# Routed results scaled by ScalarE and scattered to two token tables; a step's sum formed by accumulating transfers

## The chip, the cores and the metric

The kernel runs on one core of one Trainium2 chip. The metric is the device time of one execution in microseconds (us). Three runs of the kernel before gave a median of 2758.53 us (2753.56 to 2760.92). PE is TensorE, DVE VectorE, ACT ScalarE, POOL GpSimd, and SP the engine that here only issues transfers. A transfer issued from POOL goes through the software queue (q0 in the profile), one issued from SP through the hardware queue q1, one issued from ACT through q10.

## The reference

Two sequences of 4096 tokens, 512 features, float32. First a recurrent layer (a weight matrix `W` of 512x512 per sequence, updated after each token), a residual and a layernorm. Then a feed-forward layer with one shared and eight routed experts, a residual and a second layernorm:

```python
logits = einsum('btd,ed->bte', X, routing_W) + expert_bias
activation = sqrt(softplus(logits))
top_vals, top_idx = top_k(activation, 2)
combine = sum(one_hot(top_idx, 8) * top_vals[..., None], axis=-2)     # weight of each expert per token
y = silu(X @ rW1[e] + rb1[e]) @ rW2[e] + rb2[e]                       # for every expert e
routed = einsum('ne,end->nd', combine, y)
return layernorm(X + shared(X) + routed)
```

Each token uses two experts, so a kernel need compute only two of the eight `y`, and sum them with their weights.

## The kernel before

**Steps.** The 4096 tokens of a sequence are cut into 32 steps `c` of 128 tokens; a step holds both sequences, `B = 2`, so 256 tokens. `step(c)` (L392 on) is the recurrent layer in chunk form, with the update of `W` at L457 (matmul `pw`) and L458 (VectorE adds it to `W`), of the bias at L463 and L464 (`pb`, `brep`), and the residual at L452 and L453 (`po`, `x`). `prep(c+1)` and `invert(c)` prepare a triangular inverse: `invert` is a chain of small VectorE instructions (L347) that ends in the tiles `D` and `DT` (L364); `join` begins with a matmul `pn` that needs `D` (L376). `shared(c-1)` does the shared expert (its result added at L620) and `router(c-1)` the choice of two experts.

**Groups, tiles and tables.** Steps 0 to 22 are group a, steps 23 to 30 group b (`GROUPS = (23, 8)`); step 31 is done with all eight experts densely (`dense`, L644 to L675). For each chosen expert of each token, `router` writes the token's number (4 bytes) into one of four DRAM tables `gt` at a place that belongs to the expert (L557, four scatters of a step). At a group's end `plan` (L678) reads the tables back and cuts the pairs of token and expert into tiles of 128, 99 for group a and 39 for group b. `routed` (L759) runs over the tiles: gather 128 token rows `g` from DRAM (L766), gather the expert's weights `wb` of 1.3 MB (L772; left out by index where the buffer has them already), transpose (`pg`, L781), first layer (`phe`, L790, and ACT's silu into `he`, L794), second layer (`pye`, L801), add the bias on VectorE into `o` (L804), and write `o` with a plain SP transfer to its place in the DRAM tensor `ge` (L806), which is in order of tiles. `o` has two buffers, `g` three, `wb` three.

**Collecting.** `collect` (L827) takes one step of a group at a time: load `acc` (512 KB, shared expert plus residual, L834), gather for each of two sequences and two chosen experts the 128 result rows from `ge` into a tile `z` (256 KB each, L840), and on VectorE add each `z` times its weight `cw` to `acc` (L857). Then layernorm (`bn_stats` at L276, a square root on ACT at L281, scale and shift on ACT at L287) and the output, an ACT transfer `y_out` (L867). `plan` works out the rows of `ge` for each token, `sidx` (L732 to L744).

**Order.** Generators are interleaved by hand with `interleave`, which always resumes the part with the smallest share done. The order of PE and VectorE is exactly the order of the code; that of ACT, POOL and SP is set by a scheduler at build time. Each engine runs its own list in order, and a wait at its head holds back all that is behind it. Group a's tiles are spread over steps 24 to 27; its collection runs in steps 28 to 31, five steps in each of the first three and three in the last, and the other five beside group b's tiles. Then comes the dense expert work of step 31, with the eight collections of group b beside it:

```python
    interleave([(b.tiles * TILE, tiles[1]), (60.0, shared(NCH - 1)),
                ((a.n - sum(COLLECTED.values())) * COLLECT, collects[0])])
    dense_weights(E - len(dense_w))
    interleave([(DENSE, dense(NCH - 1)), (b.n * COLLECT, collects[1])])
```

Of the kernel before, what the change touches and what calls it, by code (L numbers as in the profile page):

```python
# [39 lines left out]
F32 = mybir.dt.float32  # L41
# [6 lines left out]
P = 128  # L48
# [5 lines left out]
K = 2  # L54
# [47 lines left out]
def postln_block(ctx: ExitStack, tc: tile.TileContext, x, xT, thK, thV, thQ, w0, b0, masks, blk,  # L102
# [24 lines left out]
    cp = ctx.enter_context(tc.tile_pool(name="cp", bufs=2))  # L127
# [99 lines left out]
    class Group:  # L227
# [9 lines left out]
        def begin(self):  # L237
            g = self.g

            def d(tag, shape):  # L240
                return dram.tile(shape, F32, tag=f"{tag}{g}", name=f"{tag}{g}", bufs=1)

            self.y, self.base = d("gy", [self.rows, D]), d("gb", [self.rows, D])

            self.tables = [d(f"gt{i}", [E * self.cap, 1]) for i in range(B * K)]
            self.ex = d("ge", [self.tiles * P, D])
            zero = plp.tile([P, E * self.cap // P], F32, tag="big", name=f"zero{g}")
            nc.vector.memset(zero, 0.0)
            for table in self.tables:
                nc.sync.dma_start(out=table.rearrange("(p n) o -> p (n o)", p=P), in_=zero)  # L250

            def t(tag, shape, dt=F32):
                return plp.tile(shape, dt, tag=f"{tag}{g}", name=f"{tag}{g}")

            i = plp.tile([P, E], I32, tag="iota", name=f"i_first{g}")
            nc.gpsimd.iota(i, pattern=[[self.cap, E]], base=0, channel_multiplier=0)
            self.first = t("first", [P, E])
            nc.vector.tensor_copy(self.first, i)
            self.next = t("next", [P, E])
            nc.vector.tensor_copy(self.next, self.first)  # L260
            self.cw = t("cw", [P, self.n, B, K])
            self.row = t("row", [P, self.n, B, K])
            self.widx = t("widx", [P, self.tiles], I32)
            self.gidx = t("gidx", [P, self.tiles], I32)
            self.sidx = t("sidx", [P, self.n, B, K], I32)
# [207 lines left out]
    def router(c, yT):  # L473
# [75 lines left out]
        for what, to in ((place, gr.row), (act, gr.cw)):  # L549
            v = small("selv", (P, B, K, E))  # L550
            nc.vector.tensor_tensor(v, sel, what[:, :, None, :].broadcast_to(full), ALU.mult)
            nc.vector.tensor_reduce(to[:, j], v, AX.X, ALU.add)
        ri = sm.tile([P, B, K], I32, tag="ri", name=f"ri_{c}")
        nc.vector.tensor_copy(ri, gr.row[:, j])  # L554
        for s in range(B):
            for k in range(K):
                nc.gpsimd.indirect_dma_start(  # L557
                    out=gr.tables[s * K + k],
                    out_offset=bass.IndirectOffsetOnAxis(ap=ri[:, s, k:k + 1], axis=0),
                    in_=code[:, j * B + s:j * B + s + 1], in_offset=None,  # L560
                    bounds_check=E * gr.cap - 1, oob_is_err=False)
# [116 lines left out]
    def plan(gr):  # L678
# [38 lines left out]
        for i in range(0, NT, half):  # L717
# [13 lines left out]

        step = tmp("step", [P, E - 1])  # L732
        nc.vector.tensor_scalar(step, tiles[:, 0:E - 1], float(P), float(-CAP),
                                ALU.mult, ALU.add)
        n = gr.n * B * K
        full = [P, n, E - 1]
        rows = gr.row.rearrange("p n s k -> p (n s k)")
        adj = tmp("big", full, "adj")
        nc.vector.tensor_tensor(adj, rows[:, :, None].broadcast_to(full),
                                gr.first[:, None, 1:].broadcast_to(full), ALU.is_ge)  # L740
        nc.vector.tensor_tensor(adj, adj, step[:, None, :].broadcast_to(full), ALU.mult)
        sl = tmp("sl", [P, n])
        nc.vector.tensor_reduce(sl, adj, AX.X, ALU.add)
        nc.vector.tensor_tensor(gr.sidx.rearrange("p n s k -> p (n s k)"), sl, rows, ALU.add)  # L744
        codes = tmp("big", [NT, B * K, P], "codes")
        for i, table in enumerate(gr.tables):
            nc.gpsimd.indirect_dma_start(
                out=codes[:, i, :], out_offset=None, in_=table.rearrange("(r n) o -> r (n o)", n=P),
                in_offset=bass.IndirectOffsetOnAxis(ap=r32[0:NT, 0:1], axis=0),
                bounds_check=E * CAP // P - 1, oob_is_err=False)  # L750
        yield 8.0
        ps = ps_f.tile([P, NT], F32, tag="pf", name=f"pc_{g}")
        for i in range(B * K):
            nc.tensor.matmul(ps, codes[:, i, :], ident[0:NT, 0:NT], start=(i == 0),
                             stop=(i == B * K - 1))
        nc.vector.tensor_copy(gr.gidx, ps)
        yield 0.2

    def routed(gr):  # L759

        NT = gr.tiles
        g_t, gT, h_t = {}, {}, {}
# [34 lines left out]
        def second(k):  # L797
# [7 lines left out]
            v = gr.order[k]  # L805
            nc.sync.dma_start(out=gr.ex[v * P:(v + 1) * P], in_=o)  # L806
# [8 lines left out]
        for k in range(NT):  # L815
            if k + NW < NT:
                tokens(k + NW)
            hidden(k)
            if k + 1 < NT:
                turn(k + 1)  # L820
            yield 2.5
            second(k)
            if k + NW < NT:
                weights(k + NW)
            yield 2.0

    def collect(gr):  # L827

        got = {}

        def fetch(j):
            c = gr.c0 + j
            acc = cp.tile([P, B, D], F32, tag="acc", name=f"acc_{c}", bufs=3)
            nc.gpsimd.dma_start(out=acc,  # L834
                                in_=gr.base[j * T:(j + 1) * T].rearrange("(s p) d -> p s d", p=P))
            z = []
            for s in range(B):
                for k in range(K):
                    t = cp.tile([P, D], F32, tag=f"z{s}{k}", name=f"z_{c}_{s}_{k}")
                    nc.gpsimd.indirect_dma_start(  # L840
                        out=t, out_offset=None, in_=gr.ex,
                        in_offset=bass.IndirectOffsetOnAxis(ap=gr.sidx[:, j, s, k:k + 1], axis=0),
                        bounds_check=gr.tiles * P - 1, oob_is_err=False)
                    z.append(t)
            got[j] = acc, z

        fetch(0)
        yield 2.0
        for j in range(gr.n):
            c = gr.c0 + j  # L850
            if j + 1 < gr.n:
                fetch(j + 1)
            acc, z = got.pop(j)
            norm = []
            for s in range(B):
                for k in range(K):
                    nc.vector.scalar_tensor_tensor(acc[:, s, :], z[s * K + k],  # L857
                                                   gr.cw[:, j, s, k:k + 1], acc[:, s, :],
                                                   ALU.mult, ALU.add)
                    yield 0.8  # L860
                norm.append(layernorm(acc, "f", c, s, scalar=True))
                next(norm[s])
                yield 0.4
                if s > 0:
                    next(norm[s - 1])
            next(norm[B - 1])
            nc.scalar.dma_start(out=out[:, c * P:(c + 1) * P, :].rearrange("s p d -> p s d"),  # L867
                                in_=acc)
# [109 lines left out]
```

## Time and profile before

| | |
|---|---|
| device time, median of three runs | 2758.53 us (2753.56 to 2760.92) |
| the profiled execution: device time, and its span from first to last instruction | 2757.97 us, 2756.0 us |
| mean granted TensorE clock of the profiled execution | 0.989 |
| busy share of the span: PE, DVE, ACT, POOL | 96%, 47%, 27%, 28% |
| group a's tiles | 1540 to 2191 us, PE busy 636.8 of 651 us |
| steps 28 to 31 with collections of group a | 2191 to 2474 us, PE busy 255.3 of 283 us |
| group b's tiles | 2474 to 2677 us, PE busy 179.5 of 203 us |
| dense experts and collections of group b | 2677 to 2756 us, PE busy 59.1 of 79 us |
| bytes moved by transfers | 269.42 MB |

The page gives busy times per engine, idle time before groups of instructions with what ended it, and for transfers the time from issue to landing. The four stretches of the table have different limits, so shares over the whole span say little about the change: it touches the last 1216 us.

### The profile page before, as it was taken

What the parts mean: (1) busy time and instruction counts of PE and PEld (TensorE: products, weight loads), DVE (VectorE), ACT (ScalarE), POOL (GpSimd) and SP (SyncE); (2) the same over time, 40 slices, a digit from 0 to 9 for tenths busy, and PEclk for the clock granted to TensorE, in tenths of its full rate; (3) what the DMA queues carried; (4) which work ended last, traced back from release to release, by engine and by line L of the source; (5) the groups of instructions that cost most, each with busy time, mean ns of one, the idle gap of its engine ahead of it and who ended that gap; (6) DMA issues with size and microseconds to landing.
All of it is one profiled execution on the core that took longest, in us unless ns stands there. A gap on an engine that the chain in (4) does not pass through costs nothing. (4 is left out here: it accounts for less than half of the span.)

```text
span 2756.0 us, 32318 instructions
## 1 busy us (share of the span) xinstructions
PE 2658.1 (96%) x10977; PEld 1718.3 (62%) x10977; DVE 1292.1 (47%) x4093; ACT 755.7 (27%) x1474; POOL 766.5 (28%) x767
## 2 busy tenths in 40 slices
PE   8999999999999999999999999999999999889887
PEld 6666666666666666666666676767667655546664
DVE  2455555444445555544445413223132388773238
ACT  1211122222221122222222322323223133334447
POOL 0121111111111111111112433243342355454445
PEclk9999999999999999999999999999999999999998
DMA  4122212111111211121112534344333467775666
GB/s 161 36 50 61 63 40 41 48 40 40 40 40 42 54 48 48 41 48 40 40 40 56 169 71 126 121 107 135 89 126 101 102 180 197 206 223 197 204 213 225
DMA packets 148787, 269.42 MB, mean 98 GB/s; under 512 B 61180, under 2 KB 62940, under 8 KB 145040
## 3 DMA queue, kind: packets, MB, share of 16 engines
q1 hardware_dynamic: 90608, 139.50, 17.5%
q0 software_dynamic: 49584, 111.61, 14.7%
q10 hardware_dynamic: 8432, 16.25, 1.7%
q8 instruction: 88, 1.44, 0.2%
q14 instruction: 75, 0.61, 0.1%
HBM read 333.37 MB, written 88.64 MB: 153 GB/s over the span
## 5 line engine op out<-in xcount | busy, mean ns | idle before, releaser
L347 DVE SCALAR_TENSOR_TENSOR X<-L,X 128x31 f32<-128x31 f32 (+22 forms) x1472 | 332.7, 274 | 27.5 <-DMA L<-dL 10.5
L557 POOL DMA_INDIRECT gt<-code,ri x124 | 123.7, 998 | 710.7 <-DVE ri L554 682.0
L790 PEld LDWEIGHTS phe<-gT,wb 128*128 128x128 f32 x2208 | 270.7, 194 | 75.4 <-issue 68.9
L804 DVE TENSOR_TENSOR o<-pye,wb 128x512 f32<-128x512 f32 x138 | 95.4, 691 | 452.1 <-PE pye L801 436.6
L790 PE MATMUL phe<-gT,wb 128*128 128x128 f32 x2208 | 273.7, 278 | 16.2 <-DMA wb<-wcat_in,widx 15.5
L801 PE MATMUL pye<-wb,he 128*128 128x512 f32 x552 | 266.8, 605 | 21.1 <-ACT he L794 20.4
L457 PE MATMUL pw<-F,K 128*128 128x512 f32 x512 | 244.6, 608 | 9.6 <-DVE W L458 8.1
L304 PE MATMUL pkq<-xT,thK 128*128 128x256 f32 x1024 | 242.9, 381 | 7.6 <-DMA thK<-thK_in 7.6
L304 PEld LDWEIGHTS pkq<-xT,thK 128*128 128x128 f32 x1024 | 195.3, 191 | 82.2 <-issue 61.6
L304 PE MATMUL pkq<-xT,thQ 128*128 128x256 f32 x1024 | 241.9, 380 | 2.6 <-ACT N L378 2.6
L422 PE MATMUL po<-W,kq 128*128 128x512 f32 x512 | 244.2, 600 | 0.0
L402 PE MATMUL pr<-thV,xT 128*128 128x512 f32 x512 | 241.8, 604 | 0.0
L407 PE MATMUL pr<-W,kq 128*128 128x512 f32 x512 | 240.1, 592 | 0.0
L772 POOL DMA_INDIRECT wb<-wcat_in,widx x138 | 141.9, 1028 | 342.9 <-DVE o L804 138.3
L304 PEld LDWEIGHTS pkq<-xT,thQ 128*128 128x128 f32 x1024 | 188.5, 191 | 40.9 <-issue 17.0
L311 ACT COPY kq<-pkq 128x256 f32<-128x256 f32 x256 | 83.2, 374 | 435.2 <-PE pkq L304 434.6
L794 ACT ACTIVATE he<-phe,wb 128x128 f32<-128x128 f32 x276 | 86.5, 363 | 419.1 <-PE phe L790 418.4
L458 DVE TENSOR_TENSOR W<-pw,W 128x512 f32<-128x512 f32 x256 | 173.4, 688 | 59.1 <-PE pw L457 56.6
L457 PEld LDWEIGHTS pw<-F,K 128*128 128x128 f32 x512 | 91.9, 191 | 141.3 <-issue 86.1
L766 POOL DMA_INDIRECT g<-gy,gidx x138 | 138.2, 1001 | 139.3 <-PE pg L781 115.0
L801 PEld LDWEIGHTS pye<-wb,he 128*128 128x128 f32 x552 | 98.6, 189 | 120.9 <-issue 76.7
L840 POOL DMA_INDIRECT z<-ge,sidx x124 | 136.5, 1101 | 100.8 <-DVE acc L857 33.9
(198 smaller groups left out, 3458.9 us busy)
## 6 DMA issues: line engine op xcount, KB each, us to landing
ge<-o SPq DMA_DIRECT2D x138, 256.0 KB, 2.0
xT<-xT_in SPq DMA_DIRECT2D x32, 512.0 KB, 3.7
x<-x_in SPq DMA_DIRECT2D x32, 512.0 KB, 3.7
L<-dL SPq DMA_DIRECT2D x128, 128.0 KB, 4.5
gy<-x SPq DMA_DIRECT2D x31, 512.0 KB, 2.8
gb<-x SPq DMA_DIRECT2D x31, 512.0 KB, 4.5
acc<-gb POOLq DMA_DIRECT2D x31, 512.0 KB, 5.2
y_out<-acc ACTq DMA_DIRECT2D x31, 512.0 KB, 6.0
```

The source lines that it names most:

```text
L304: nc.tensor.matmul(ps[:, i].rearrange("p s t -> p (s t)"), th[:, dc, (ec + i) * P:(ec + i + 1) * P], xt[:, dc].rearrange("p s t -> p (s t) ...
L347: nc.vector.scalar_tensor_tensor(X[:, h, j + 1:], L[:, j + 1:, j], X[:, h, j:j + 1], X[:, h, j + 1:], ALU.mult, ALU.add)
L402: nc.tensor.matmul(ps, xt[:, dc, s, :], nthV_sb[:, dc, :], start=(dc == 0), stop=False)
L407: nc.tensor.matmul(ps, KQ[:, ec, s, 0, :], W[s][:, ec, :], start=False, stop=(ec == DC - 1))
L422: nc.tensor.matmul(ps, KQ[:, ec, s, 1, :], W[s][:, ec, :], start=(ec == 0), stop=False)
L457: nc.tensor.matmul(ps, K[s][:, ec, :], F[s], start=True, stop=True)
L458: nc.vector.tensor_tensor(W[s][:, ec, :], ps, W[s][:, ec, :], ALU.add)
L766: nc.gpsimd.indirect_dma_start(out=g_t[k], out_offset=None, in_=gr.y, in_offset=bass.IndirectOffsetOnAxis(ap=gr.gidx[:, k:k + 1], axis=0), ...
L772: nc.gpsimd.indirect_dma_start(out=wbuf[k % NW], out_offset=None, in_=wcat, in_offset=bass.IndirectOffsetOnAxis(ap=gr.widx[:, k:k + 1], ax ...
L790: nc.tensor.matmul(ps[:, hc, :], w[:, dc * HF + hc * P:dc * HF + (hc + 1) * P], t[:, dc, :], start=(dc == 0), stop=(dc == DC - 1))
L801: nc.tensor.matmul(ps, h[:, hc, :], w[:, O2 + hc * D:O2 + (hc + 1) * D], start=(hc == 0), stop=(hc == HC - 1))
L840: nc.gpsimd.indirect_dma_start(out=t, out_offset=None, in_=gr.ex, in_offset=bass.IndirectOffsetOnAxis(ap=gr.sidx[:, j, s, k:k + 1], axis=0 ...
```

## The change

The second number in the table `gt`, the weight of the token's expert, travels with the token's number (8 bytes instead of 4), and `plan` reads both back, so that each tile knows for its 128 rows the weight (`cw`, one column for a tile) and the destination row (`sidx`). After the bias is added, ACT multiplies `o` by its weight in place, and POOL scatters the 128 rows to `ge`, which now holds two tables in token order, one for the first and one for the second chosen expert. `collect` no longer gathers: the two halves of `ge` for a step are contiguous, and two POOL transfers of 512 KB add them to `acc` as they are written (`accum_op=ADD`). Loads run up to three steps ahead, with five `acc` buffers instead of three; the eight `z` buffers are gone. The four instructions of `plan` over all tokens of a group (L739 to L744) are gone as well.

```diff
-    cp = ctx.enter_context(tc.tile_pool(name="cp", bufs=2))
+    cp = ctx.enter_context(tc.tile_pool(name="cp", bufs=5))
...
-            self.tables = [d(f"gt{i}", [E * self.cap, 1]) for i in range(B * K)]
-            self.ex = d("ge", [self.tiles * P, D])
+            self.tables = [d(f"gt{i}", [E * self.cap, 2]) for i in range(B * K)]
+            self.ex = d("ge", [K * self.rows, D])
...
             for table in self.tables:
-                nc.sync.dma_start(out=table.rearrange("(p n) o -> p (n o)", p=P), in_=zero)
+                for r in table.rearrange("(h p n) o -> h p (n o)", h=2, p=P):
+                    nc.sync.dma_start(out=r, in_=zero)
...
-        for what, to in ((place, gr.row), (act, gr.cw)):
+        row = small("row", (P, B, K))
+        entry = sm.tile([P, B, K, 2], F32, tag="entry", name=f"entry_{c}")
+        for what, to in ((place, row), (act, entry[:, :, :, 1])):
...
+        for k in range(K):
+            nc.vector.tensor_scalar(entry[:, :, k, 0], code[:, j * B:(j + 1) * B],
+                                    float(k * gr.rows + 1), None, ALU.add)
...
-                    in_=code[:, j * B + s:j * B + s + 1], in_offset=None,
+                    in_=entry[:, s, k, :], in_offset=None,
...
-        ps = ps_f.tile([P, NT], F32, tag="pf", name=f"pc_{g}")
-        for i in range(B * K):
-            nc.tensor.matmul(ps, codes[:, i, :], ident[0:NT, 0:NT], start=(i == 0),
-                             stop=(i == B * K - 1))
-        nc.vector.tensor_copy(gr.gidx, ps)
+        ps = ps_f.tile([P, 2, NT], F32, tag="pf", name=f"pc_{g}")
+        for v in range(2):
+            for i in range(B * K):
+                nc.tensor.matmul(ps[:, v], codes[:, i, :, v], ident[0:NT, 0:NT], start=(i == 0),
+                                 stop=(i == B * K - 1))
+        nc.vector.tensor_copy(gr.cw, ps[:, 1])
+        off = tmp("wr", [P, NT], "off")
+        nc.vector.tensor_scalar(off, ps[:, 0], 0.0, float(SKIP), ALU.is_equal, ALU.mult)
+        nc.vector.scalar_tensor_tensor(gr.sidx, ps[:, 0], -1.0, off, ALU.add, ALU.add)
...
             nc.vector.tensor_tensor(o, ps, w[:, OB2:OB2 + D], ALU.add)
-            v = gr.order[k]
-            nc.sync.dma_start(out=gr.ex[v * P:(v + 1) * P], in_=o)
+            nc.scalar.mul(o, o, gr.cw[:, k:k + 1])
+            o_t[k] = o
+
+        def results(k):
+            o = o_t.pop(k)
+            nc.gpsimd.indirect_dma_start(
+                out=gr.ex, out_offset=bass.IndirectOffsetOnAxis(ap=gr.sidx[:, k:k + 1], axis=0),
+                in_=o, in_offset=None, bounds_check=K * gr.rows - 1, oob_is_err=False)
...
             hidden(k)
+            if k > 0:
+                results(k - 1)
...
         def fetch(j):
+            if j + 3 < gr.n:
+                c = gr.c0 + j + 3
+                acc[j + 3] = cp.tile([P, B, D], F32, tag="acc", name=f"acc_{c}")
+            for r, i in enumerate((j + 3, j + 2, j + 1)):
+                if not 0 <= i < gr.n:
+                    continue
+                src = gr.base if r == 0 else gr.ex[(r - 1) * gr.rows:r * gr.rows]
+                nc.gpsimd.dma_start(out=acc[i], accum_op=ALU.add if r else ALU.bypass,
+                                    in_=src[i * T:(i + 1) * T].rearrange("(s p) d -> p s d", p=P))
+        for j in range(-3, 0):
+            fetch(j)
+            yield 2.0
         for j in range(gr.n):
             c = gr.c0 + j
-            if j + 1 < gr.n:
-                fetch(j + 1)
-            acc, z = got.pop(j)
+            fetch(j)
+            t = acc.pop(j)
             norm = []
             for s in range(B):
-                for k in range(K):
-                    nc.vector.scalar_tensor_tensor(acc[:, s, :], z[s * K + k],
-                                                   gr.cw[:, j, s, k:k + 1], acc[:, s, :],
-                                                   ALU.mult, ALU.add)
-                    yield 0.8
-                norm.append(layernorm(acc, "f", c, s, scalar=True))
+                norm.append(layernorm(t, "f", c, s, scalar=True))
                 next(norm[s])
-                yield 0.4
...
```

## The prediction

> **What bounds it now.** TensorE: 2658.1 of 2756.0 us busy. An edit elsewhere pays only where PE waits, so I asked first for busy time by stretch (columns: width, busy PE, PEld, DVE, ACT, POOL, clock, DMA share, GB/s), cut where the kernel's stages begin.
>
> ```profile
> 1540.00:2191.00 651.00, 636.83 (x3268) 450.01 (x3266) 177.78 (x499) 186.28 (x417) 230.15 (x230) 0.99 0.39 110
> 2268.00:2335.00 67.00, 62.34 (x224) 37.57 (x223) 56.21 (x171) 26.32 (x48) 36.06 (x35) 0.97 0.73 190
> 2410.00:2474.00 64.00, 51.28 (x157) 27.19 (x158) 50.71 (x167) 17.78 (x30) 32.09 (x32) 0.89 0.68 212
> 2474.00:2677.00 203.00, 179.46 (x994) 126.20 (x993) 60.03 (x138) 89.09 (x172) 99.20 (x97) 0.99 0.62 212
> 2677.00:2756.00 79.00, 59.12 (x192) 36.38 (x190) 60.73 (x148) 57.72 (x80) 40.17 (x38) 0.89 0.67 216
> ```
>
> Group a's tiles (first row) leave PE 14 us idle in 651. Steps 28 to 31 are where VectorE is full (56 of 67 us), group b's tiles lose 24 us, the end 20. Next, PE's waits in steps 28 to 31:
>
> ```profile
> PE pw L457 <- DVE W L458: 8.1, 7, 1.9
> PE pn L376 <- DVE D L364: 5.7, 1, 5.7
> PE pt L576 <- DVE x L289: 4.0, 1, 4.0
> PE pb L463 <- DVE W L458: 3.4, 2, 2.6
> PE pw L457 <- DVE x L453: 1.5, 3, 0.6
> ```
>
> All five end on VectorE, 22.7 us together; its timeline there has L857 pairs (1.53 us) between the updates of W. In group b's tiles the list is different:
>
> ```profile
> PE pye L801 <- ACT he L794: 16.6, 15, 1.9
> PE phe L790 <- DMA wb<-wcat_in,widx: 5.0, 4, 2.2
> ```
>
> Those are ACT's table reloads (1.28 us) between square root and silu, and weights that land late. Then the transfers: landing times on the page, and the chain that ended last.
>
> ```profile
> ge<-o SPq DMA_DIRECT2D x138, 256.0 KB, 2.0
> acc<-gb POOLq DMA_DIRECT2D x31, 512.0 KB, 5.2
> g<-gy,gidx POOLq DMA_INDIRECT x138, 3.5
> z<-ge,sidx POOLq DMA_INDIRECT x124, 5.1
> ```
>
> ```profile
> 2677.68 1.95 DMA ge<-o
> 2683.19 5.13 DMA z<-ge,sidx
> 2702.99 6.84 DMA acc<-gb
> 2750.75 1.52 ACT acc L287 x2
> ```
>
> The end already hangs on transfers: last tile's write, first gathers, loads, the last normalization. I sum against the profiled execution, 2757.97 us (span 2756.0), 0.6 below the median of 2758.53, and count 8.3 us (0.3%) as the least that a measurement tells from no change.
>
> **Steps 28 to 31: -18.** L857 goes, 124 x 0.743 = 92 us of VectorE, 18 steps of four here: 54 us out of VectorE's 229 in this stretch. Of the 22.7 us I take back the W group whole (8.1 + 3.4 + 1.5 = 13.0) and half of the other two (9.7/2 = 4.9). It holds only if each `acc` is summed when VectorE comes to its statistics, since a late one now holds all of VectorE and soon PE. In POOL's new list an `acc` passes through load, first add, second add, each waiting for the landing before it: L per adding transfer, G per plain one. I laid the list on the old step (2268 to 2335): the load of step 8 goes out at 2286, after the copy of X, its sum is complete at 2286 + G + 2L + 1, and VectorE asks near 2326, since the three-step lead moved its work back. G + 2L may be 39 us. I count no loss here. Bounds: 0 to -27 (all 22.7 and some clock; 0.89 was granted after the long stalls).
>
> **Group a's tiles: 0.** A tile gains a scale on ACT (0.80 us, the row of L287, same shape) and a scatter on POOL (1.00 + 0.30 between issues), and each scatter waits for the one before it to land, as they write the same tensor. A landing like g's, 3.5 us, makes a chain of 3.8 per tile; a tile takes 651/99 = 6.6. POOL goes from 230 to 359 us of 651. If ACT is held by a late `o`, `he` and `gT` stand behind it: ACT idles 3.7 to 5.7 us before each `he` here, which covers it; without that cover 99 x 0.8 = 79 us. SP loses 138 issues of 0.32 us that waited 519.8 us for `o`; PE waits here for no tile that SP loads, so nothing. Bounds -3 to +10.
>
> **Group b's tiles: +13.** Less cover: a tile alone takes 4.23 us of PE, 203/39 = 5.2 with the waits. POOL has 3 x 1.3 = 3.9 us of issues for a tile. The chain: g's median here is 3.9, so 4.2. That is the edge; I take 0.15 x 20 tiles = +3. A scatter behind a weight load waits for it (the load on the last chain took 8.73 us, a g behind one 7.67), POOL stands, and the next load goes out late: four late loads now, I take +6. The scale sits between a square root and the silu reload in five of ten places of ACT's list: 5 x 0.8 = +4. Gathers of group a that leave POOL here (18 fewer issues) are in this. Bounds 0 to +25. At this place the Trainium skill, "ScalarE: Activation LUTs", section "Rules for kernel authors", says to multiply on VectorE, not on ScalarE; by it the +4 would vanish, 39 x 0.74 us would go to an engine busy 60 of 203 us, and the sum would be 4 lower.
>
> **Plan, router, tables: +2.5.** Two more rounds of `pc` matmuls, 16 rows, four of which took 0.63 us: +2.5. `plan` on VectorE loses 2.7 us in group a (0.82, 0.83, 0.82, 0.25) and gains five small ones; 62 small ones in the router (0.15 each) lie in steps where PE waited 4.0 us for VectorE in 1540. Eight more SP issues for zeros and 8-byte scatters (same count, 0.998 each) are behind other work: 0, at most +3.
>
> **The end: +9.** VectorE's last `o` ends at 2677.66; scale 0.80, scatter 3.9: 2682.4. The first `acc` needs two adds: 2682.4 + 2L. From statistics to y_out the old run took 8.5 us (2687.09 to 2695.61), landing 5.9: its buffer is free at 2696.8 + 2L. There are eight steps and five buffers, so the last three loads wait for outputs, and POOL's list has them strictly one after another: load, add, add; load, add, add; load, add, add. A unit is G + L + 1.7 (two gaps of 0.3, one issue of 1.1), and the last add must land: 2696.8 + 2L + 3(G + L) + 4.0 + L. Then two statistics (1.4) and the old run's 6.0 from the last one (2749.99) to the end: 2708.2 + 6L + 3G. G = 5.2 (page). L is not in the trace: an add also reads its target. Rows: 512 KB plain took 4.2 in 2200 to 2300, 256 KB 3.4, so 0.8 for 256 KB and 1.6 for another 512 KB: L = 6.8. That gives 2764.6, +8.6. Bounds: L = G = 5.2 gives 2755.0 (-1); a whole transfer more, L = 10.4, gives 2786 (+30). Below, ACT is the floor: 19.7 of 20 us busy in 2700 to 2720, so not under about -4. VectorE's saving there (32 x 0.743 = 24 us) buys nothing: dense work advances at ACT's 8 us per expert. The Trainium skill, "DMA: Bandwidth & Descriptors", section "Anatomy of one DMA — SWDGE (gpsimd) path", puts a transfer of this path at 2.0 us plus bytes over 436 GB/s, an estimate of 3.2 us for 512 KB; with that for L and G the walk would end at 2737 and ACT would set the end; this trace shows no 512 KB load under 4.1, so it is not used.
>
> **Sum.** 2757.97 - 18 + 0 + 13 + 2.5 + 8.6 = 2764.1.
>
> **Rivals.** *Adds cost what loads cost* (L about 5.2): -1 or less at the end, -20 in the steps, +5 in the tiles, since shorter transfers clear the ring: -15, 2743. For it: landings of 4.2 in steps 28 to 31, and the dense stage moves less in parallel. Against: an add moves its bytes twice, and the DMA share at 2700 to 2720 was already 0.89. *Adds cost double* (L = 10.4): the end becomes +30, the steps still hide it (26 < 39), sum -18 + 13 + 2.5 + 30 = +27.5, 2785. Its place is the row of nine transfers at the end; it decides from L = 7.2, where the sum passes +8.3. *The scatters' chain becomes group b's bound*: at z's 5.1 it is 5.4 per tile, 8 us over 203; at 5.9, 6.2 x 39 = 242, +39, which with the rest of the sum is near 2785 to 2795; it decides from 4.9 (203/39 less 0.3). For it: one ring now carries g, wb, scatters and adds. Against: g's 3.9. *Nothing moves*: the steps' waits have other causes and the end is ACT's either way: 2758.
>
> **Chances.** The forecast 0.36 (own range 2750 to 2775; by the bound faster 0.04, same 0.19, slower 0.13), cheap adds 0.26 (0.23, 0.03, 0), double adds 0.25 (0, 0.01, 0.24), the chain 0.09 (all slower), nothing 0.04 (same). Together faster 0.27, same 0.27, slower 0.46. The range 2736 to 2792 cuts off the outer part of the cheap and of the double case, about a tenth each.
>
> **What would show it.** After: an adding transfer's landing time near 6.8 (5.2 or 10.4 settle the first two rivals); PE's waits for VectorE in steps 28 to 31 near 5 instead of 22.7; in group b's tiles PE waits for `wb` near 11 and POOL waits that end on a scatter; at the end loads and adds of the last three steps in single file on POOL, with VectorE and ACT idle between them, and PE done well before the last output. I am wrong in kind if statistics in steps 28 to 31 wait for an add, or if PE waits for ACT behind a scale in group a's tiles.

## The result, and the profile after

The changed kernel takes 2801.4 us (median of four runs, 2796.96 to 2808.99) against 2759.73 for the kernel before in the same runs: ratio 1.015 [1.0134, 1.0167], 1.5% slower. The forecast was 2764.1 with a range of 2736 to 2792. The profiled execution took 2804.95 us, span 2803.2. (One of the four executions of `move_x`, a kernel of the table below, took 12659 us; it is left out of that kernel's numbers.)

Nearly the whole loss lies behind group a's tiles. These are three stretches of the kernel after, cut at the end of the last `pye` of group a, the first `pg` of group b, the first `pd` of the dense work and the end (columns: width, busy PE, PEld, DVE, ACT, POOL, clock, DMA share, GB/s):

```profile
2194.60:2480.90 286.30, 251.81 (x878) 149.94 (x878) 180.95 (x635) 97.20 (x176) 106.06 (x101) 0.94 0.79 186
2480.90:2706.80 225.90, 189.10 (x992) 131.07 (x991) 46.36 (x116) 115.43 (x211) 129.59 (x126) 0.93 0.59 183
2706.80:2803.20 96.40, 60.04 (x193) 36.31 (x191) 38.33 (x121) 60.05 (x84) 24.87 (x23) 0.84 0.76 180
```

Cut at the same places, the kernel before has 281.1, 202.4 and 79.2 us with PE busy 253.8, 178.9 and 59.3. So the account of the 47.2 us between the two spans is +1.3 up to the last tile of group a, +5.2 in steps 28 to 31, +23.5 in group b's tiles, +17.2 at the end. VectorE has lost 49 us in the first stretch (229.8 to 181.0); 54 were forecast. PE's waits in steps 28 to 31, in the same window (2191 to 2474) as in the list before:

```profile
PE pn L377 <- issue: 18.8, 1, 18.8
PE pn L377 <- DVE D L365: 9.5, 2, 5.1
...
PE pb L464 <- DVE W L459: 1.1, 3, 0.4
...
PE pw L458 <- DVE W L459: 0.5, 1, 0.5
```

The waits around `W` that the change should remove are gone: 13.0 us before, 1.6 now. The other two, 9.7 us before (`pn` 5.7, `pt` 4.0), are 10.6 now (9.5 and 1.1). And one new wait of 18.8 us, before `pn` in step 31, is larger than what was won. It is put down to "issue", so the timelines must say who was late. `pn` began at 2452.19 and needs `D`. VectorE first, then POOL in the 30 us ahead of it:

```profile
2444.04 0.69 DVE L627 TENSOR_TENSOR x<-py,x 128x512 f32<-128x512 f32 x1 [15.11 <-POOL x L595]
...
2451.62 0.42 DVE L365 TENSOR_TENSOR D<-C,blk 128x256 f32<-128x256 f32 x1
```

```profile
2415.02 1.35 POOL L853 DMA_DIRECT2D acc<-gb  x1
...
2424.66 1.21 POOL L853 DMA_DIRECT2D acc<-ge  x1 [7.53 <-DMA acc<-gb]
2425.40 1.22 POOL L853 DMA_DIRECT2D acc<-gb  x1
2426.16 1.76 POOL L415 TENSOR_TENSOR x<-x,brep 128x512 f32<-128x512 f32 x1
2430.98 1.20 POOL L853 DMA_DIRECT2D acc<-ge  x1 [3.06 <-DMA acc<-ge]
2432.92 1.20 POOL L853 DMA_DIRECT2D acc<-ge  x1 [0.74 <-DMA acc<-gb]
2433.66 1.75 POOL L415 TENSOR_TENSOR x<-x,brep 128x512 f32<-128x512 f32 x1
2441.51 1.20 POOL L853 DMA_DIRECT2D acc<-ge  x1 [6.09 <-DMA acc<-ge]
2442.26 2.96 POOL L595 TENSOR_TENSOR x<-x,b 128x512 f32<-128x512 f32 x2
```

POOL stands at each add until the transfer before it into the same `acc` has landed (7.53, 3.06, 0.74, 6.09 us), and behind the last add stands `x<-x,b`, an addition of the step itself. VectorE waits 15.11 us for it, then does `plan`'s small instructions, and so makes `D` only at 2451.62; PE waits for that. In group b's tiles gathers `g` and weights `wb` are late:

```profile
PE pye L805 <- ACT he L798: 16.9, 14, 3.1
PE pg L785 <- DMA g<-gy,gidx: 9.4, 2, 8.0
PE phe L794 <- DMA wb<-wcat_in,widx: 6.0, 3, 3.6
```

The kernel before had 16.6, 0.8 and 5.0 us in these three rows. The longer wait for `g` (7.96 us, until 2503.62) has the same cause as the one in step 31: POOL issued that gather behind two adds at which it had stood.

```profile
2493.21 1.18 POOL L853 DMA_DIRECT2D acc<-ge  x1 [6.94 <-DMA acc<-gb]
2495.82 1.17 POOL L853 DMA_DIRECT2D acc<-ge  x1 [1.43 <-DMA acc<-ge]
2497.30 1.10 POOL L770 DMA_INDIRECT g<-gy,gidx  x1 [0.30 <-issue]
```

The longest wait for `wb` (3.64 us, until 2616.29) has another: POOL had not stood ahead of that load. It went out at 2606.62, right behind a load and an add of `acc` (2604.25, 2604.99), and took 9.53 us to land. A load of weights on the last chain of the kernel before took 8.73, so the adds need not be the cause.

PE idles 36.8 us in this stretch instead of 23.5, and it is also busy 10.2 us longer with the same matmuls, at a clock of 0.93 instead of 0.99. The PE timeline shows how: after the wait of 3.64 us the next sixteen matmuls took 3.75 us, where an earlier group of sixteen took 1.95.

```profile
2608.26 1.95 PE L794 MATMUL phe<-gT,wb 128*128 128x128 f32 x16
...
2616.29 3.75 PE L794 MATMUL phe<-gT,wb 128*128 128x128 f32 x16 [3.64 <-DMA wb<-wcat_in,widx]
```

The granted clock was 0.97 from 2600 to 2616, 0.52 from 2616 to 2622 and 1.00 from there to 2640. Such a stall is paid twice, as idle time and as slow matmuls behind it. (The Trainium skill, "TensorE: Matmul & The Clock Gate", section "Part 1: The HAM clock gate", describes a clock that is halved when PE has idled and released after some microseconds of work; these rows agree, 0.52 behind the wait and 1.00 six us later.) The chain that ended last now runs through the loads and adds of the last steps (from each issue to the landing):

```profile
2733.35 9.78 DMA acc<-ge
...
2744.20 6.68 DMA acc<-gb
...
2758.25 8.27 DMA acc<-gb
...
2774.07 7.71 DMA acc<-gb
...
2789.42 5.79 DMA acc<-ge
...
2797.76 1.52 ACT acc L288 x2
```

### The profile page after: what moved, and what is told of

It is laid out like the page before. It is cut to its first block, busy times and chain, and to the rows that moved or that the text cites. A ratio compares the mean times of both kernels' runs of the same rounds, so it can differ in the third digit from the quotient of the medians.

```text
span 2803.2 us, 32304 instructions
## 1 busy us (share of the span) xinstructions
PE 2668.8 (95%) x10993; PEld 1722.9 (61%) x10993; DVE 1208.3 (43%) x4031; ACT 856.8 (31%) x1615; POOL 848.7 (30%) x843
## 5 line engine op out<-in xcount | busy, mean ns | idle before, releaser
L564 POOL DMA_INDIRECT gt<-entry,ri x124 | 123.4, 995 | 710.7 <-DVE ri L561 680.9
L794 PEld LDWEIGHTS phe<-gT,wb 128*128 128x128 f32 x2208 | 271.0, 194 | 70.2 <-issue 59.7
L805 PE MATMUL pye<-wb,he 128*128 128x512 f32 x552 | 274.0, 619 | 29.3 <-ACT he L798 23.2
L809 ACT ACTIVATE o<-o,cw 128x512 f32<-128x512 f32 x138 | 99.5, 721 | 286.3 <-DVE o L808 265.2
L814 POOL DMA_INDIRECT ge<-o,sidx x138 | 142.0, 1029 | 100.5 <-issue 53.7
```

The lines of the kernel that those rows point to most:

```text
L794: nc.tensor.matmul(ps[:, hc, :], w[:, dc * HF + hc * P:dc * HF + (hc + 1) * P], t[:, dc, :], start=(dc == 0), stop=(dc == DC - 1))
L805: nc.tensor.matmul(ps, h[:, hc, :], w[:, O2 + hc * D:O2 + (hc + 1) * D], start=(hc == 0), stop=(hc == HC - 1))
L814: nc.gpsimd.indirect_dma_start(out=gr.ex, out_offset=bass.IndirectOffsetOnAxis(ap=gr.sidx[:, k:k + 1], axis=0), in_=o, in_offset=None, bou ...
```

## The experiments

Two theories at first. Queue theory: POOL's list stands still between loads and adds, and what is behind them is late. Transfer theory: adding transfers are dear by themselves. A third, tile theory, blames scale and scatter for group b's tiles. All results first; lengths are of one profiled execution each, cut as above. The kernel before ran with median 2759 to 2763 us beside most of them and 2745 beside `one_add`, `sp_load_dve` and `hybrid2`, so kernels are compared by their ratios to it. `no_adds`, `one_add` and `plain_chain` leave a part of the sum out of the output; they only show what that part costs.

| kernel | median us | ratio to before | steps 28-31 | group b's tiles | end |
|---|---|---|---|---|---|
| before | | 1 | 281.1 | 202.4 | 79.2 |
| the change | 2801.4 | 1.0150 [1.0134, 1.0167] | 286.3 | 225.9 | 96.4 |
| move_x | 2802.1 | 1.0159 [1.0129, 1.0190] | 285.7 | 224.6 | 97.2 |
| no_adds | 2737.5 | 0.9915 [0.9888, 0.9942] | 256.6 | 212.5 | 77.5 |
| one_add | 2736.9 | 0.9972 [0.9959, 0.9986] | 264.8 | 204.2 | 77.3 |
| plain_chain | 2752.7 | 0.9961 [0.9948, 0.9974] | 270.7 | 208.2 | 80.5 |
| pool_code_order | 2834.3 | 1.0265 [1.0239, 1.0292] | 325.4 | 222.2 | 89.1 |
| sp_load | 2774.4 | 1.0038 [1.0019, 1.0057] | 266.5 | 223.1 | 88.8 |
| sp_load_dve | 2748.1 | 1.0013 [0.9996, 1.0029] | 265.4 | 210.8 | 89.4 |
| o5 | 2805.1 | 1.0173 [1.0147, 1.0199] | 291.0 | 226.4 | 93.4 |
| scale_dve | 2809.6 | 1.0169 [1.0152, 1.0186] | 286.5 | 227.8 | 97.8 |
| sums_vec | 2758.6 | 0.9995 [0.9983, 1.0006] | 271.0 | 221.4 | 78.8 |
| sums_scale_vec | 2750.3 | 0.9961 [0.9946, 0.9976] | 270.0 | 204.6 | 79.5 |
| pool_loads | 2789.2 | 1.0101 [1.0073, 1.0129] | 284.4 | 225.9 | 81.6 |
| scatter_add | 2775.6 | 1.0046 [1.0029, 1.0063] | 254.3 | 242.8 | 78.1 |
| hybrid | 2797.2 | 1.0114 [1.0084, 1.0145] | 316.4 | 206.3 | 79.0 |
| hybrid2 | 2720.0 | 0.9908 [0.9879, 0.9937] | 258.3 | 192.5 | 78.4 |

**move_x: the step's own additions off POOL.**

```diff
-            nc.gpsimd.tensor_tensor(xc[:, s, :], xc[:, s, :], brep[s], ALU.add)
+            eng = nc.vector if c >= NCH - 4 else nc.gpsimd
+            eng.tensor_tensor(xc[:, s, :], xc[:, s, :], brep[s], ALU.add)
```

(and `x<-x,b` of the same steps to VectorE, just ahead of L627)

> The changed kernel, but in steps 28 to 31 the two POOL additions x<-x,brep and x<-x,b (two instructions each) are done by VectorE, so no arithmetic of the step stands behind an adding transfer in POOL's list. Queue theory (POOL's list stands still behind loads and adds, and what is behind them is late): the wait of 18.8 us before pn in step 31 goes and the first tile of group b starts some 13 us earlier, near 2467; VectorE gets about 16 x 0.7 = 11 us, which it has free; time 2786 to 2790. Rival, transfer theory (the adds' traffic is slow wherever it is issued and something waits for it in any order): the wait only moves to the statistics fst<-acc, the tiles start near 2480 and the time stays within 2797 to 2805.

The wait before `pn` went, `pn` of step 31 began at 2426.6 instead of 2452.2, and nothing was gained. PE's longest wait:

```profile
PE pc L753 <- DMA codes<-gt,r: 18.5, 3, 17.4
```

Now `pc`, the first matmul of the plan for group b, waits 17.4 us: the last table writes `gt` and readings `codes` stand in the same list behind the same adds. The number expected by the queue theory was wrong, since only one of the two things behind the line had been counted, and the rival's numbers (2797 to 2805) came out. Its mechanism did not: the wait moved not to the statistics but to the next thing on POOL, and that whatever comes next on POOL is late is what the row shows.

**no_adds, one_add: how much do adds cost?** `no_adds` leaves out both adds of a step, `one_add` the second.

```diff
-            for r, i in enumerate((j + 3, j + 2, j + 1)):
+            for r, i in enumerate((j + 3,)):              # one_add: (j + 3, j + 2)
```

> The changed kernel without its two adding transfers of each step (the routed result is left out of the output); scale, scatter and plain loads stay. Queue theory: steps 28 to 31 end about 20 us earlier (281 -> 263 us), group b's tiles lose the 9.4 us of late g and some of the slow clock behind it (226 -> 212), and the end is ACT's alone (96 -> 76): 2745 to 2752. Rival, tile theory (scale on ACT, two buffers of o and the chain of scatters are the cost in group b's tiles): the tiles stay at 222 to 228 and the time at 2757 to 2765.

> The changed kernel with one adding transfer of each step instead of two (the results of the second chosen expert are left out of the output). Rate theory (load and add in single file take about 8.5 + 6.7 = 15 us at worst and 12 where the load is not held up, near the 13.4 us that a step leaves for each of five sums; only the excess costs): most of the loss goes, 2740 to 2760, end 78 to 84 us. Theory of a cost in proportion to the number of adds: half way between none (2737) and two (2801), 2765 to 2775.

From none to one the ratio rises by 0.0057, from one to two by 0.0178, three times as much. That is no cost per transfer; the second add passes a limit. The steps show it (256.6, 264.8, 286.3 us) and the end too (77.5, 77.3, 96.4); in the tiles (212.5, 204.2, 225.9) the first add even comes with a fall, which is not explained. So the cost in proportion to the number of adds, expected by the one theory, did not come, and the limit expected by the other did. Without adds, and so without the sum, what is left of the change is 0.85% faster than the kernel before: the loss comes in with the adds. (Tile theory's number for `no_adds`, tiles of 222 to 228 us, did not come: with scale and scatter alone they take 212.5.)

**plain_chain: the same list, without the adding.**

```diff
-                nc.gpsimd.dma_start(out=acc[i], accum_op=ALU.add if r else ALU.bypass,
+                nc.gpsimd.dma_start(out=acc[i], accum_op=ALU.bypass,
```

> The changed kernel with its two adding transfers of each step turned into plain ones into the same acc (the sum is left out: the last table overwrites the rest). Order of POOL's list, targets, sources and the wait of each transfer for the one before it are the same; only the adding is gone. Queue theory (the waiting in line costs, whatever a transfer does): POOL's waits for acc<-gb and acc<-ge stay near 122 us in steps 28 to 31, only the landing gets shorter by what adding costs, 1 to 2 us each: 2780 to 2797. Transfer theory (adding is what is dear): back to the kernel without adds, 2737 to 2755.

POOL's list is the same instruction by instruction, and the loss is gone: 0.9961, the number that the transfer theory expected (2752.7 us), not the queue theory's 2780 to 2797. POOL still waits for landings, but 84 us instead of 120, where the queue theory had them stay. Its waits between 2195 and 2450, first of the changed kernel, then of this one:

```profile
POOL acc L853 <- DMA acc<-gb: 64.2, 13, 9.7
POOL acc L853 <- DMA acc<-ge: 55.9, 13, 8.1
```

```profile
POOL acc L853 <- DMA acc<-gb: 56.3, 14, 8.8
...
POOL acc L853 <- DMA acc<-ge: 28.1, 10, 4.6
```

The adding makes each turn in the line longer. How long a transfer holds the line is best read at the end, where little else is on POOL. The changed kernel, then plain_chain:

```profile
2758.25 1.21 POOL L853 DMA_DIRECT2D acc<-gb  x1
2766.80 1.16 POOL L853 DMA_DIRECT2D acc<-ge  x1 [7.34 <-DMA acc<-gb]
2773.36 1.17 POOL L853 DMA_DIRECT2D acc<-ge  x1 [5.40 <-DMA acc<-ge]
2774.07 1.20 POOL L853 DMA_DIRECT2D acc<-gb  x1
2782.76 1.16 POOL L853 DMA_DIRECT2D acc<-ge  x1 [7.48 <-DMA acc<-gb]
2789.42 1.18 POOL L853 DMA_DIRECT2D acc<-ge  x1 [5.50 <-DMA acc<-ge]
```

```profile
2711.72 0.71 POOL L853 DMA_DIRECT2D acc<-gb  x1
2717.38 0.71 POOL L853 DMA_DIRECT2D acc<-ge  x1 [4.94 <-DMA acc<-gb]
2721.27 0.71 POOL L853 DMA_DIRECT2D acc<-ge  x1 [3.18 <-DMA acc<-ge]
2721.97 0.71 POOL L853 DMA_DIRECT2D acc<-gb  x1
2727.82 0.71 POOL L853 DMA_DIRECT2D acc<-ge  x1 [5.14 <-DMA acc<-gb]
2732.79 0.71 POOL L853 DMA_DIRECT2D acc<-ge  x1 [4.26 <-DMA acc<-ge]
```

From issue to the next issue in the chain, an add takes 6.56 and 6.66 us, a plain transfer in its place 3.89 and 4.97. The plain load ahead of it takes 8.55 and 8.69 beside adds, 5.66 and 5.85 beside plain ones. From load to load that is 15.8 against 10.3 us (2758.25 to 2774.07, 2711.72 to 2721.97). In steps 28 to 31, five sums share a step of 67 us in the trace of before, 13.4 us for each: plain transfers in single file (10.3) stay under that, a load and two adds (15.8) do not. The steps' own rows agree. From 2274.74 to 2425.40 the changed kernel issues eleven plain loads 15.1 us apart, and POOL waits 0.57 us in all for a free buffer (`acc<-gb` behind `y_out<-acc`): it is never ahead. The same eleven loads are 13.9 us apart in plain_chain (2262.54 to 2401.81) and 13.8 in one_add (2252.53 to 2390.17), where POOL waits 9.8 and 26.7 us for free buffers: there the line is ahead of the steps. The pages give a median from issue to landing for adds only in one_add, here with its plain loads:

```profile
acc<-gb POOLq DMA_DIRECT2D x31, 512.0 KB, 7.1
acc<-ge POOLq DMA_DIRECT2D x31, 512.0 KB, 6.9
```

(The Trainium skill, "Collectives: The Full Stack", section "The bandwidth ceiling: the fold count and why AG ≠ RS ≠ AR", says of ReduceScatter, a collective between cores, that it is slower than AllGather for the second source read of its addition, not for the adding, with a measured ratio of 1.93. Inside this kernel 6.6 stands to some 4.4, about 1.5; no run here separates the second read from the addition.)

**sp_load: the plain load out of the line.**

```diff
-                nc.gpsimd.dma_start(out=acc[i], accum_op=ALU.add if r else ALU.bypass,
+                kw = dict(accum_op=ALU.add) if r else {}
+                (nc.gpsimd if r else nc.sync).dma_start(out=acc[i], **kw,
```

> The changed kernel with the plain load of acc issued by SP instead of POOL; the adds stay in POOL's list. POOL no longer stands for y_out (19 us in steps 28 to 31) and the loads of the last three steps can go out as soon as their buffer is free. Queue theory: two thirds of the line remain (add after add, tables and gathers behind them), step 31 still stalls for 10 us and more; the end falls from 96 to 86-90: 2778 to 2792. Transfer theory: nothing but the end moves by a few us, 2793 to 2803.

A better result than either expectation: 1.0150 becomes 1.0038, and the steps take 266.5 us, 20 less, without the long wait in step 31. All the adds are still made. So in the steps it is neither the adds alone nor the queue alone: it is the sum of what stands in single file on POOL for one result, set against the 13.4 us that a step leaves for it. Two adds without the load are 13.2 us by the spacing above, at the limit, and this kernel shows no long stall. Each of three edits that shorten the line (one add, plain transfers, no load) takes most of the loss in the steps away. The end keeps a part of its loss (88.8), group b's tiles most of it (223.1).

**pool_code_order: the same instructions, POOL in the order of the code.**

```diff
-    ctx.enter_context(tc.manual_schedule(engines={mybir.EngineType.PE, mybir.EngineType.DVE}))
+    ctx.enter_context(tc.manual_schedule(engines={mybir.EngineType.PE, mybir.EngineType.DVE,
+                                                  mybir.EngineType.Pool}))
```

> The changed kernel with the same instructions, but POOL too runs them in the order in which the code is written (before, a scheduler set it): of each step's three transfers the load leads the first add by one step and the first add the second, so that a transfer seldom follows the one that it has to wait for, and step 31's table writes and readings stand ahead of its last adds. Queue theory (the adds cost because POOL stands still between them): waits of POOL for acc<-gb and acc<-ge in steps 28 to 31 fall from 122 us to below 40, the wait before pn and pc in step 31 goes, the end loses its single file (96 -> 80 to 86): 2745 to 2770. Transfer theory (the adds' own length and traffic cost it, in any order): waits and time stay, 2790 to 2805.

Both expected times failed; it is the slowest kernel of all. POOL's waits for landings did fall as expected, from 120 us to 25, but now the adds are late, because POOL stands for the step's own work ahead of them. From its waits between 2195 and 2520, POOL's and then VectorE's:

```profile
POOL gt L564 <- DVE ri L561: 59.0, 4, 26.5
...
POOL acc L853 <- DMA acc<-ge: 15.2, 5, 4.2
...
POOL acc L853 <- DMA acc<-gb: 9.8, 5, 3.7
```

```profile
DVE fst L277 <- DMA acc<-ge: 49.6, 5, 14.7
```

VectorE's statistics wait 49.6 us for sums, and PE 43.6 us for VectorE. Neither of the two orders serves both: adds first, and the step's tables and additions are late; the step first, and the sums are.

**The tiles: o5, scale_dve, sums_vec, sums_scale_vec, sp_load_dve.** `o5` gives `o` five buffers; `scale_dve` has VectorE multiply; `sums_vec` keeps scale and scatter but forms the sums on VectorE from plain SP loads; the other two combine these.

```diff
-            o = gp.tile([P, D], F32, tag="o", name=f"o_{gr.g}_{k}")
+            o = gp.tile([P, D], F32, tag="o", name=f"o_{gr.g}_{k}", bufs=5)              # o5
-            nc.scalar.mul(o, o, gr.cw[:, k:k + 1])
+            nc.vector.tensor_scalar(o, o, gr.cw[:, k:k + 1], None, ALU.mult)             # ..._dve, sums_scale_vec
-                nc.gpsimd.dma_start(out=acc[i], accum_op=ALU.add if r else ALU.bypass,
+                    nc.sync.dma_start(out=t, in_=gr.ex[r:r + P])                         # sums_...: z, 256 KB
...
+                    nc.vector.tensor_tensor(acc[:, s, :], z[s * K + k], acc[:, s, :], ALU.add)
```

> The changed kernel with five buffers of o instead of two, so VectorE does not wait for a scatter to have read its o (33.7 us in seven waits in group b's tiles). Tile theory: group b's tiles go from 226 to 205-212, time 2783 to 2790. Queue theory: the late g and late wb stay, since POOL still stands behind adds and the scatters still follow one another; 2 to 6 us gained: 2795 to 2800.

> The changed kernel with o multiplied by its weight on VectorE (a 128x512 tensor_scalar, 0.55 us as in L290) instead of on ACT. Theory that ACT's list is held by the scale (it waits up to 4.7 us for o, and gT and he stand behind it): PE's waits for he in group b's tiles fall from 16.9 us to below 9 and the tiles from 226 to 212-218: 2786 to 2794; in group a's tiles nothing. Queue theory alone: the adds in POOL's list decide, 2797 to 2803.

> The first half of the change alone: scale and scatter to token order as in the changed kernel, but each step's sum is formed by VectorE from plain loads (acc 512 KB, four z of 256 KB) that SP issues; no adding transfer, nothing of the collection on POOL. Queue theory: steps 28 to 31 as in the kernel before (281), group b's tiles 205 to 213, end 79 to 82: 2760 to 2770. Tile theory: group b's tiles stay near 226, with DVE waiting some 30 us for scatters: 2778 to 2785. Transfer theory: adds were the slow part, so also 2760 to 2770.

> The half with the scale and the scatter, sums formed by VectorE from plain loads on SP, and also the scale on VectorE. Group b's tiles took 221 us with the scale on ACT, with 24.5 us of PE waiting for he. ACT-list theory: these waits return to the 16.6 of the kernel before, the tiles to 205-212, time 2744 to 2752, faster than both kernels. Rival (the scatter chain and POOL's 3.9 us of issues per tile are the limit): tiles stay at 218 to 223, time 2755 to 2762.

> Adds on POOL, plain load on SP, and o scaled on VectorE. ACT-list theory: with the load off POOL's list the wait of ACT for o is what is left in group b's tiles, which go from 223 to 208-214 us: 2758 to 2767. Rival (late g and wb behind the adds in POOL's list are what is left): tiles 219 to 225 and 2771 to 2778, as the scale on VectorE gained nothing in the changed kernel itself.

With five buffers VectorE no longer waits for scatters (33.7 us in the changed kernel, none now) and the tiles take 226.4 us, as ever, so neither theory's gain came. ACT now stands longer at its scale for `o` (31.9 us in the changed kernel):

```profile
ACT o L809 <- DVE o L808: 78.1, 36, 3.8
```

Tile theory in the form "buffers of `o`" falls. In `scale_dve` moving the scale alone gains nothing either (1.0169): PE waits 22.0 us for `he`, not below 9 as expected, and 11.0 for `g`. `sums_vec` went against the queue theory: without any add its tiles still take 221.4 us, not 205 to 213, though its steps (271.0) and end (78.8) are as good as or better than before. There the scale is what counts: 221.4 to 204.6 us from `sums_vec` to `sums_scale_vec` (PE's waits for `he` 24.5 to 16.6), and 223.1 to 210.8 from `sp_load` to `sp_load_dve`, both as the theory of ACT's list expected. So group b's tiles have at least two costs: the adds, behind which `g` is late on POOL, and the scale in ACT's list. How they combine stays open: with one add and the scale on ACT (`one_add`) the tiles take 204.2 us.

**pool_loads: POOL's list without chains.** As `sums_vec`, but the loads (512 KB, acc and two z) are issued by POOL.

```diff
-                    nc.sync.dma_start(out=t, in_=gr.ex[r:r + P])
+                nc.gpsimd.dma_start(out=t, in_=gr.ex[r:r + T].rearrange("(s p) d -> p s d", p=P))
```

> The same three transfers of 512 KB for a step, all issued by POOL, but plain and into three tiles of their own (acc and two z), which VectorE sums; scale on ACT as in the changed kernel. No transfer follows one into the same tile before VectorE has read it. Queue theory in the form that the waits for a landing are what hold POOL: POOL waits for buffers alone and the time is that of the sums from SP's loads, 2757 to 2772. Rival: 1.5 MB of POOL's transfers for a step and their issues are dear in any form: 2785 to 2805.

The rival was right in its number: 1.0101 against 0.9995 with SP's loads. POOL now waits for VectorE to free its `z` (33.9 us) and for outputs to free `acc` (35.7) between 2195 and 2450, and PE waits for `W` again (14.3 us), as before the change. So here plain transfers that have to wait for something cost on a list that holds other work, too, not only adds.

**scatter_add, hybrid, hybrid2: the add in the scatter.** The scatter itself adds to `gb`; padding rows go behind the table.

```diff
-                out=gr.ex, out_offset=bass.IndirectOffsetOnAxis(ap=gr.sidx[:, k:k + 1], axis=0),
-                in_=o, in_offset=None, bounds_check=K * gr.rows - 1, oob_is_err=False)
+                out=gr.base, out_offset=bass.IndirectOffsetOnAxis(ap=gr.sidx[:, k:k + 1], axis=0),
+                in_=o, in_offset=None, bounds_check=gr.rows + P - 1, oob_is_err=True,
+                compute_op=ALU.add)
```

> The sum without collecting transfers: each tile's scaled o is added by its scatter itself to its tokens' rows of the table gb, which holds shared expert plus residual (padding rows go to 128 rows behind the table); a step then needs one plain load of 512 KB, on SP. No adding transfer waits for another one in a step's chain, but every scatter now adds. Queue theory: like the kernel without adds, if a scatter that adds lands as one that writes (3 to 4 us): 2737 to 2752. Transfer theory (an adding transfer is dear by itself): the scatter chain takes over group b's tiles, at 6 us and more for each of 39 tiles, 235 us and above, and 99 tiles of group a approach 6.6 us each: 2765 to 2800.

> Group a by scatters that add into the table gb (hidden under 6.6 us per tile there; steps 28 to 31 took 254 us so), group b by plain scatters and sums on VectorE from SP's loads with the scale on VectorE (tiles 205, end 79.5). Steps 254 instead of 270 with the rest as in the best kernel so far: 2741 - 16 in the profile, median 2728 to 2738. Rival: the adding scatters hold VectorE's o or POOL in group a's tiles as they did in group b's (6.2 us each), and 5 to 20 us are lost there: 2740 to 2755.

> Group a by scatters that add into gb, one plain load for each of its steps on SP, its steps spread as before (in the first form of this kernel all of its steps came in one bunch, since a step without sums counted as shorter); group b by plain scatters and sums on VectorE, where the first load of a step is the table that the last scatter completes, so that no load of group b stands early in SP's list. Steps 28 to 31 near 254 us, tiles 203 to 208, end 79 to 80: 2725 to 2740, faster than the sums on VectorE alone (2750). Rival: adding scatters (6.2 us each in group b's tiles) cost group a's tiles 10 us and more: 2742 to 2755.

In `scatter_add` the steps (254.3) and the end (78.1) are those of a kernel without adds, and group b's tiles become a chain of adding scatters, 242.8 / 39 = 6.2 us each, as the transfer theory expected. VectorE's waits there:

```profile
DVE o L805 <- DMA gb<-o,sidx: 139.9, 27, 10.4
```

Group a's tiles, 6.6 us each, hide the same chain: they end at 2195.9, against 2194.6 in the changed kernel. `hybrid` therefore uses it for group a alone and sums on VectorE for group b; its first form missed both expectations and lost 62 us against `scatter_add` in the steps (316.4). There a step without sums counted 0.8 instead of 4.0 in the interleaving, and SP's loads for group b stood early in its list; `hybrid2` changes both (which of them cost more was not separated) and is, of the kernels with the whole sum, the fastest: 0.9908 [0.9879, 0.9937], 0.9% faster than the kernel before. Its tiles (192.5) are shorter than the 203 to 208 expected, and nothing here was run to say why.

## Why the prediction was wrong, point by point

- **Direction and size.** Slower by over 0.3% had the largest chance (0.46), but the time predicted was 5.6 us above the median before, and the range ended at 2792. Measured: 41.7 us between the medians.
- **Steps 28 to 31: -18 forecast, +5.2 measured. This is the step that failed.** Most of the part taken back was right: the waits around `W` fell from 13.0 to 1.6 us, while the half of the other two waits did not come (9.7 to 10.6), and `sp_load`, which keeps the adds, gets 14.6 of the 18 us. "I count no loss here" was wrong. It compared a latency, G + 2L, with a lead of 39 us. What counts in a line that is never ahead is its rate: three transfers in single file took 15.1 us for each sum, where a step leaves 13.4. And the only waiting instruction asked about was VectorE's statistics. They indeed waited for no add in steps 28 to 31, so this sign of being wrong in kind did not appear; what was late were the additions of the step, the table writes and the gathers that stand behind the adds in the same list, and their delay was put at nothing. POOL's single file was named for the end and its waits for the tiles; for the steps it was not, though their own POOL work stands in the same list.
- **Group a's tiles: 0 forecast, +1.3 measured.** Right, with some luck: 1.1 of it was there when the first `pye` began, and inside the tiles 10.5 us of waits for `wb`, which the prediction did not count, went, while others came (PE for `he` 3.8 to 6.3 us, one of 3.8 put down to "issue", `py` for VectorE 1.9).
- **Group b's tiles: +13 forecast, +23.5 measured.** Of its terms, the scatters' chain (+3) was not needed: taking VectorE's wait for it away (o5) gained nothing. Late weights (+6) came mostly as late `g` (9.4 us against 0.8) and hardly as `wb` (6.0 against 5.0). The scale on ACT (+4) was undersized for two kernels: taking it off ACT gained 12 and 17 us there, and nothing in the changed kernel itself. No term stood for the slow clock behind the stalls; PE was busy 10.2 us longer.
- **Plan, router, tables: +2.5 forecast.** The `pc` matmuls of group a took 1.0 us longer (1.03 to 2.02); nothing more of this term can be told apart in the traces.
- **The rule against the scale on ACT.** The Trainium skill, "ScalarE: Activation LUTs", section "Rules for kernel authors", was weighed at 4 us in favour of VectorE. One pair of runs agrees with its advice clearly (0.9995 to 0.9961), a second with intervals that overlap (1.0038 to 1.0013), the changed kernel itself does not (1.0150 to 1.0169). One scale takes 0.72 us on ACT and 0.49 on VectorE; beside that ACT stood 50.8 us for `o` in group b's tiles of `sums_vec`, in front of `he`. Which of the two counted was not separated.
- **The end: +8.6 forecast, +17.2 measured.** The single file of the last three steps is there as forecast. L = 6.8 was close (median 6.9 in one_add; 5.79 and 9.78 in the chain, 6.6 from issue to issue). G = 5.2 was the term that was mis-sized: 6.68, 8.27 and 7.71 in the chain, 7.1 us more for the three loads, each of which goes out 0.7 to 0.8 us behind an add. That is not quite the 8.6 us missing: from the issue of the first of them to the landing of the last add 51.0 us passed and 46.8 were forecast, since the adds among them were shorter than 6.8; another 3.8 were lost before, the file beginning 37.4 us after the first `pd` instead of 33.6.
- **The rivals.** "Adds cost double" had the right order of time (2785) for a wrong place: not the end alone. Its L of 10.4 is not the rule (median 6.9, below its point of decision of 7.2), though single adds took 9.78 us at the end and 11.54 in the tiles, from 2483.77. The scatters' chain did not become the bound. Cheap adds did not come either. No rival was the one that happened: POOL's list as the bound in the steps.

## What to carry to other kernels

Before moving work from an engine to transfers, add up what the issuing engine's list must do in single file for one result, each transfer at its landing time, and set that against the time that one result has; here 15.1 us against 13.4 made the later instructions of the list late. Ask of each waiting issue not only who reads its result but what stands behind it. Take what can go elsewhere out of the full list (the load moved to SP: 1.0150 to 1.0038), or put the addition where a chain is hidden anyway (group a's scatters: 0.9908).

## What the runs showed of the hardware that was not expected

The profile's record of an adding transfer's issue on POOL is longer too. These are the issues in the changed kernel and the same ones in plain_chain (ns: least, median, most):

```profile
L853 POOL DMA_DIRECT2D acc<-ge x62: 1157/1201/2210, 2198.7 to 2789.4; - x62
```

```profile
L853 POOL DMA_DIRECT2D acc<-ge x62: 709/715/827, 2196.3 to 2732.8; - x62
```

1.20 us against 0.72. Not all of it delays the list: in both kernels a plain load began 0.7 us after the issue ahead of it (2773.36 and 2774.07, 2721.27 and 2721.97). Three issues into `acc<-ge` in a row took 3.76 us (from 2713.58) and 2.20 (from 2678.09 in plain_chain). And the add's neighbours are slower: from its issue to the next one, a plain load of 512 KB took 8.55 and 8.69 us beside an add and 5.66 and 5.85 beside a plain transfer, so the price of an add is not all in its own row. A scatter of 128 rows that adds made a chain of 6.2 us per tile; in hybrid2 the median from issue to landing is 4.8 us for it and 2.8 for a plain one.
